# Feed-forward of six batches moved between the attention heads of later batches, with weight preparation in three batches, x in per-batch tiles, and silu written with tanh

## The chip, the cores and the metric

The kernel runs on one core of one Trainium2 chip. The metric is device time in microseconds (us), the median of the runs shown. A profiled execution gives a span (first to last instruction) and the trace that all views below come from.

## The reference

Eight batches of 256 rows, 512 channels, 16 heads of 32 channels; a context of 256 rows per batch. A cross-attention block with int8-like quantised projections, then a feed-forward (FFN) block with fp8-like quantised linears and two reorder indices. Cut to what matters:

```
x = x + tanh(g_xattn) * xattn(layernorm(x), ctx, mask, wq, bq, wk, bk, wv, bv, wo, bo)
x = x + tanh(g_ffn)   * ffn(layernorm(x), w_gate, w_up, w_down, up_idx, down_idx)

xattn: q = w8a8(x, wq, bq); k = ctx @ wk.T + bk; v = ctx @ wv.T + bv   # 16 heads
       o = softmax(q k^T / sqrt(32) + mask) v;  return w8a8(o, wo, bo)
w8a8:  rows of x and of w divided by their absmax/127 and rounded, product rescaled
ffn:   qx = fp8(x[:, up_idx] / row scale); g, u = qx @ fp8(W[:, up_idx]).T, rows in down_idx order
       t = silu(g) * u;  qt = fp8(t[:, down_idx] / row scale);  y = qt @ fp8(w_down[:, down_idx]).T
```

The FFN is 512 to 1408 (gate and up) to 512.

## The kernel before

All rows stand in 16 row tiles of 128 (two per batch). The kernel has three stages.

**Prologue.** SP loads context, mask, wk, x, wv, wq, wo; all eight batches of x go into one resident tile `x_sb`. The constants come on ACT's queue, the two gates last. `held_up` builds a 0/1 mask of the columns that `up_idx` names; wk and wv are turned on PE (`prep_fp32`), wq and wo are quantised and turned (`prep_int8`). `project_kv` and `project_q` make keys, values and queries of batch 0. POOL gathers `dd_i` (the doubled index) and marks the columns that `down_idx` names by 11 scattered writes into one DRAM table, `held_d` (`mark_down`, L341).

**Attention.** A loop over 8 batches of 8 steps (two heads a step) plus 8 more steps. Each step runs three parts at lags 0, 1 and 2: `scores` (PE L538; then per head and row tile a fused add-mask-and-minimum on DVE, L553, and an exponential on ACT, L563), `transposed` (four fp32 PE transposes a head, L579, and a copy out of PSUM on DVE L588 or ACT L586) and `products` (PE L597, a copy, a turn back, a scaling on DVE L620). Beside these, `slots` receive other work by `spread`: the next batch's context turns, keys, values and queries (their bias add on POOL, L505), the output projection of the batch before (`project_out`; y on DVE L666, two adds into `x_sb` on POOL L669 and L670), the second layernorm and its quantisation (`quantise_x2`, stored to DRAM as `scr_x`), the layernorm statistics of all later batches (in batch 0), and the "pieces": 11 row blocks each of w_gate and w_up (`prep_up`), 4 of w_down (`prep_down`) and the gathers that reorder them through DRAM. The pieces are spread over seven batches. Attention's PSUM is one 4-bank tile for the scores and 4 single banks (`bank`) for everything else.

**Feed-forward.** After the attention pools are closed, a plain loop over 8 batches and two row tiles. POOL gathers the batch's turned rows (`xg`, L834). For each half of the 1408 columns: 16 gate and up matmuls of 352 columns each (L850) into two-bank PSUM tiles; DVE scales gate and up (704 wide, L863 and L872); ACT takes Silu (L881); POOL multiplies into `tt` (L882). Then DVE takes the row's absmax over 1408 (L187), the row is put on the fp8 grid (`fp8_grid`: two ACT passes L165 and L167, two DVE passes L169 and L170), PE turns it (L894), ACT copies it out (L897), 11 matmuls make `yp` (L900), DVE scales (L906), POOL adds x (L907), SP stores. The tiles of this stage have two buffers each.

The queues are not in the order of the source: the language orders each engine's queue by priorities and its own estimates (the mask load of the FFN weights, last in its list of pieces, is issued at 70.1 us). `nc.any` copies go to ACT or DVE by the same choice.

Of the kernel before, what the change touches and what calls it, by code (L numbers as in the profile page):

```python
# [40 lines left out]
P = 128  # L41
# [10 lines left out]
def tile_flamingo_block(  # L52
# [49 lines left out]
    x_sb = ctile([P, NT, C], "x_sb")  # L102

    def load_x(b):
        nc.sync.dma_start(
            x_sb[:, b * TPB : (b + 1) * TPB, :], x[b].rearrange("(t p) c -> p t c", p=P)
        )

    d_i = ctile([P, IC], "d_i", I32)
    nc.scalar.dma_start(d_i, down_idx.rearrange("(k p) -> p k", p=P))  # L110
    u_i = ctile([P, KC], "u_i", I32)
    nc.scalar.dma_start(u_i, up_idx.rearrange("(k p) -> p k", p=P))
# [8 lines left out]
    gate = ctile([P, 2], "gate")  # L121
    nc.scalar.dma_start(gate[:, 0:1], g_xattn.partition_broadcast(P))
    nc.scalar.dma_start(gate[:, 1:2], g_ffn.partition_broadcast(P))
# [27 lines left out]
    md_b = ctile([P, I], "md_b", BF16)  # L151
    mx2 = ctile([P, NT], "mx2")
    var2 = ctile([P, NT], "var2")
# [5 lines left out]
    held_d = dram.tile([I, 1], F32, tag="held_d", name="held_d")  # L159
    scr_x = [dram.tile([C, S], BF16, tag=f"scr_x{b}", name=f"scr_x{b}") for b in range(B)]  # L160

    def fp8_grid(rp, src, rs, dst, n, name):

        v = rp.tile([P, n], F32, tag="r_v", name=f"v_{name}")
        nc.scalar.activation(v, src, AF.Identity, scale=rs)  # L165
        a = rp.tile([P, n], FP8, tag="r_a", name=f"a_{name}")
        nc.scalar.activation(a, v, AF.Abs, scale=0.5, saturate=False)  # L167
        q = rp.tile([P, n], FP8, tag="r_q", name=f"q_{name}")
        nc.vector.tensor_scalar(q, v, F8_MAX, -F8_MAX, ALU.min, ALU.max, saturate=False)  # L169
        nc.vector.scalar_tensor_tensor(dst, a, F8_MAX / 2, q, ALU.max, ALU.mult)  # L170
# [18 lines left out]
    with ExitStack() as actx:  # L189
# [4 lines left out]
        rp = actx.enter_context(tc.tile_pool(name="rp", bufs=2))  # L194
        one = actx.enter_context(tc.tile_pool(name="one", bufs=1))
# [4 lines left out]
        def bank(name, dt=F32):  # L200
# [4 lines left out]
        mv1 = wp.tile([P, NT, 2], F32, tag="mv1", name="mv1")  # L205
        rstd1, nmean1, sx, rsx, qa, qb = (
            wp.tile([P, NT], F32, tag=n, name=n)
            for n in ("rstd1", "nmean1", "sx", "rsx", "qa", "qb")
        )

        def norm_stats(t):
            st = sm.tile([P, 6], F32, tag="st", name=f"st1_{t}")
            nc.vector.bn_stats(st, x_sb[:, t, :])
            nc.vector.bn_aggr(mv1[:, t, :], st)

        def norm_rstd(t0, t1):
            ts = slice(t0, t1)
            nc.vector.tensor_scalar(rstd1[:, ts], mv1[:, ts, 1], LN_EPS, None, ALU.add)
            nc.scalar.activation(rstd1[:, ts], rstd1[:, ts], AF.Sqrt)
            nc.vector.reciprocal(rstd1[:, ts], rstd1[:, ts])  # L220
            nc.vector.tensor_scalar(nmean1[:, ts], mv1[:, ts, 0], -1.0, None, ALU.mult)

        def norm_max(t):
            xc = rp.tile([P, C], F32, tag="r_v", name=f"xc_{t}")
            nc.scalar.activation(xc, x_sb[:, t, :], AF.Identity, bias=nmean1[:, t : t + 1])
            absmax(sx[:, t : t + 1], xc)

        def norm_scales(t0, t1):
            ts = slice(t0, t1)
            nc.vector.tensor_tensor(sx[:, ts], sx[:, ts], rstd1[:, ts], ALU.mult)  # L230
            nc.vector.tensor_scalar(sx[:, ts], sx[:, ts], R127, Q_EPS, ALU.mult, ALU.max)
            nc.vector.reciprocal(rsx[:, ts], sx[:, ts])
            nc.vector.tensor_tensor(qa[:, ts], rsx[:, ts], rstd1[:, ts], ALU.mult)
            nc.vector.tensor_tensor(qb[:, ts], qa[:, ts], nmean1[:, ts], ALU.mult)

        def norm_steps(t0, t1):
            steps = [partial(norm_stats, t) for t in range(t0, t1)]
            steps += [partial(norm_rstd, t0, t1)]
            steps += [partial(norm_max, t) for t in range(t0, t1)]
            return steps + [partial(norm_scales, t0, t1)]  # L240
# [32 lines left out]
        def round_int8(src, rs, dst, name):  # L273
            w = rp.tile([P, C], F32, tag="r_w", name=f"ri_{name}")
            nc.vector.tensor_scalar(w, src, rs, MAGIC, ALU.mult, ALU.add)
            nc.vector.tensor_scalar(dst, w, -MAGIC, None, ALU.add)
# [45 lines left out]
        def held_up():  # L322

            iota = one.tile([P, C], F32, tag="xm", name="iota")
# [13 lines left out]

        def mark_down(k):

            nc.gpsimd.indirect_dma_start(  # L341
                out=held_d[:, :],
# [5 lines left out]
        def load_down_marks():  # L348
            md_f = one.tile([P, I], F32, tag="wd", name="md_f")
            nc.sync.dma_start(md_f, held_d.rearrange("c e -> (c e)").partition_broadcast(P))  # L350
            nc.vector.tensor_copy(md_b, md_f)
# [28 lines left out]
        def prep_down(k):  # L380
            wr = one.tile([P, I], F32, tag="wd", name=f"wd_{k}")
            nc.sync.dma_start(wr, w_down[k * P : (k + 1) * P, :])
            nc.vector.tensor_tensor(wr, wr, md_b, ALU.mult)
# [80 lines left out]
        def project_q(b):  # L464
# [4 lines left out]
            def rows():  # L469
                pt = bank(f"qt_{b}", BF16)  # L470
                for nt in range(TPB):
                    t = b * TPB + nt
                    xc = rp.tile([P, C], F32, tag="r_v", name=f"xq_{t}")
                    nc.scalar.activation(  # L474
                        xc,
                        x_sb[:, t, :],
                        AF.Identity,
                        bias=qb[:, t : t + 1],
                        scale=qa[:, t : t + 1],
# [10 lines left out]
                row_bcast(sxb, sx[:, b * TPB : (b + 1) * TPB], f"sx{b}")  # L490
# [20 lines left out]
        def attention(b, qT, kT, v, mk):  # L511
# [4 lines left out]
            o = kv.tile([P, TPB, C], F32, tag="o", name=f"o_{b}")  # L516
# [11 lines left out]
            def scores(i):  # L528
# [18 lines left out]
                for h in heads:  # L547
                    sn = at.tile([P, TPB, L], F32, tag="sn", name=f"sn_{b}_{h}")
                    pr = at.tile([P, TPB, L], F32, tag="pr", name=f"pr_{b}_{h}", bufs=6)
# [84 lines left out]
        def project_out(b, o):  # L634
# [19 lines left out]
            def product(nt):  # L654
# [10 lines left out]
                y = rp.tile([P, C], F32, tag="r_v", name=f"y_{t}")  # L665
# [3 lines left out]
                nc.gpsimd.tensor_tensor(x_sb[:, t, :], x_sb[:, t, :], bo_b, ALU.add)  # L669
                nc.gpsimd.tensor_tensor(x_sb[:, t, :], x_sb[:, t, :], y, ALU.add)  # L670
# [3 lines left out]
        def quantise_x2(b):  # L674

            xT = one.tile([P, KC, S], BF16, tag="x2T", name=f"x2T_{b}")

            def rows(nt):
                t = b * TPB + nt
                st = sm.tile([P, 6], F32, tag="st", name=f"st2_{t}")  # L680
                nc.vector.bn_stats(st, x_sb[:, t, :])
                mv = sm.tile([P, 2], F32, tag="mv", name=f"mv2_{t}")
                nc.vector.bn_aggr(mv, st)
                nc.vector.tensor_copy(var2[:, t : t + 1], mv[:, 1:2])
                xm = one.tile([P, C], F32, tag="xm", name=f"xm_{t}")
                nc.vector.scalar_tensor_tensor(
                    xm, x_sb[:, t, :], mv[:, 0:1], mu_b, ALU.subtract, ALU.mult
# [3 lines left out]
                rs = scale_of(sm, mx, mx2[:, t : t + 1], f"x2_{t}")  # L691
# [9 lines left out]

        cr, mk = load_batch(0)
        rows_k = load_halves("k", wk, "o")
        load_x(0)
        rows_v = load_rows("v", wv, "pT", 6)
        rows_q = load_rows("q", wq, "pr", 6)
        two = one.tile([P, 2, C], F32, tag="wd", name="wr_o01")
        nc.sync.dma_start(two, wo[: 2 * P, :].rearrange("(k p) c -> p k c", p=P))
        rows_o = [two[:, 0, :], two[:, 1, :]]
        for k in (2, 3):  # L710
            wr = ld.tile([P, C], F32, tag="wr", name=f"wr_o{k}", bufs=2)
            nc.sync.dma_start(wr, wo[k * P : (k + 1) * P, :])
            rows_o.append(wr)
        for b in range(1, B):
            load_x(b)
        held_up()
        prep_fp32("k", rows_k)
        for f in norm_steps(0, TPB):
            f()
# [22 lines left out]
        nc.gpsimd.dma_start(held_d.rearrange("(k p) e -> p (k e)", p=P), zeros)  # L742

        def gate_piece(k):
            mark_down(k)
            prep_up("gate", w_gate, k)

        pieces = [partial(gate_piece, k) for k in range(IC)]
        pieces += [partial(gather_up, "gate")]
        pieces += [partial(prep_up, "up", w_up, k) for k in range(IC)]  # L750
        pieces += [partial(gather_up, "up"), load_down_marks]
        pieces += [partial(prep_down, k) for k in range(KC)] + [gather_down]

# [6 lines left out]

        parts = {}
        for g in range(B * NP + NP):
            b, i = divmod(g, NP)
            if i == 0:
# [3 lines left out]
                if b == 0:  # L768
                    spread(slots, norm_steps(TPB, NT), 0, 4)
                    spread(slots, [out_scales], 5, 6)  # L770
                if b + 1 < B:
                    cr, mk = load_batch(b + 1)
                    kT, v, kv_steps = project_kv(b + 1, cr)
                    qT, q_steps = project_q(b + 1)
                    spread(slots, kv_steps, 0, 6)
                    spread(slots, q_steps, 4 if b == 0 else 3, 7)
                if b > 0:
                    spread(slots, project_out(b - 1, o_last) + quantise_x2(b - 1), 2, NP)
                if b < B - 1:
                    n0, n1 = (len(pieces) * k // (B - 1) for k in (b, b + 1))  # L780
                    spread(slots, pieces[n0:n1], 4 if b == 0 else 0, NP)
# [6 lines left out]


    with ExitStack() as fctx:  # L790
        fp = fctx.enter_context(tc.tile_pool(name="fp", bufs=1))
        fx = fctx.enter_context(tc.tile_pool(name="fx", bufs=3))
        fw = fctx.enter_context(tc.tile_pool(name="fw", bufs=2))
        fs = fctx.enter_context(tc.tile_pool(name="fs", bufs=4))
        ps_g = fctx.enter_context(tc.tile_pool(name="ps_g", bufs=1, space=PSUM))
        ps_q = fctx.enter_context(tc.tile_pool(name="ps_q", bufs=2, space=PSUM))
        ps_y = fctx.enter_context(tc.tile_pool(name="ps_y", bufs=2, space=PSUM))

        def row_bcast_f(dst, cols, name):
# [160 lines left out]
```

## Time and profile before

| | us |
|---|---|
| median of 3 runs (751.19 to 754.42) | 753.54 |
| profiled execution, device time | 751.51 |
| its span | 749.7 |
| mean granted TensorE clock | 0.869 |

| engine | busy us | instructions |
|---|---|---|
| PE (matmul) | 529.4 | 3565 |
| DVE (vector) | 550.4 | 1437 |
| ACT (scalar) | 415.6 | 956 |
| POOL (GpSimd) | 272.2 | 237 |

The first scores of the attention run on PE at 55.06 us, the last exponential starts at 495.8, the first FFN matmul at 521.3 and the last store is issued at 741.0. Busy time is the union of an engine's instructions; "idle before X, released by Y" says what ended a gap.

### The profile page before, as it was taken

The page shows a single profiled execution, that of the slowest core. Times are in us where ns is not written, and L with a number is a line of the kernel's source. Part 1 is how long each engine was busy: PE and PEld are TensorE (multiplying, and loading weights), DVE is VectorE, ACT ScalarE, POOL GpSimd, SP SyncE. Part 2 cuts the span into 40 slices and gives each one's busy share as a digit, 9 for nine tenths or more (in the row PEclk, how much of TensorE's full clock was granted, in tenths as well). Part 3 has the DMA queues.
Part 4 walks back from the last instruction along what each step waited for, and adds up shares of the span by engine and source line. Part 5 has one row for each costly group of instructions (what it writes and reads, how often), then busy time and mean ns, then how long its engine had stood idle before and what let it go on. Part 6 is the DMA issues. An engine that isn't in the chain of part 4 may idle for free. (4 is left out here: it accounts for less than half of the span.)

```text
span 749.7 us, 10414 instructions
## 1 busy us (share of the span) xinstructions
PE 529.4 (71%) x3565; PEld 341.6 (46%) x3588; DVE 550.4 (73%) x1437; ACT 415.6 (55%) x956; POOL 272.2 (36%) x237
## 2 busy tenths in 40 slices
PE   1637877878967787887867765643857767777762
PEld 1524645646646545555545444431634434444421
DVE  2755978699797788797689873755567676968971
ACT  1436877768657658678486553552235444545550
POOL 5154046035144224131301115104455576655440
PEclk9879888989989889989998888766689899989985
DMA  8931112002043012012311123000100010000000
GB/s 242 239 108 41 68 43 85 1 29 86 1 138 115 15 41 73 2 46 89 120 53 39 40 78 92 1 15 14 43 14 32 25 42 29 33 24 29 29 14 28
DMA packets 26853, 42.32 MB, mean 56 GB/s; under 512 B 6352, under 2 KB 13904, under 8 KB 26800
## 3 DMA queue, kind: packets, MB, share of 16 engines
q1 hardware_dynamic: 18512, 28.91, 12.0%
q0 software_dynamic: 4704, 12.21, 5.7%
q10 hardware_dynamic: 3584, 0.54, 0.5%
q8 instruction: 28, 0.46, 0.2%
q14 instruction: 25, 0.20, 0.1%
HBM read 31.02 MB, written 10.63 MB: 56 GB/s over the span
## 5 line engine op out<-in xcount | busy, mean ns | idle before, releaser
L563 ACT ACTIVATE pr<-sn,nm 128x256 f32<-128x256 f32 x256 | 128.4, 506 | 51.0 <-DVE nm L553 39.0
L553 DVE CUSTOM_DVE_ANT_0 sn<-s,mk 128x256 f32<-128x256 f32 x256 | 98.4, 417 | 24.4 <-issue 9.5
L579 PE MATMUL t<-ident,pr 128*128 128x128 f32 x512 | 83.8, 314 | 11.3 <-DVE pT L588 4.2
L850 PEld LDWEIGHTS <-xg 128*128 128x128 bf16 x512 | 52.6, 104 | 74.7 <-issue 35.0
L882 POOL TENSOR_TENSOR tt<-up,sl 128x704 f32<-128x704 f32 x32 | 62.9, 1966 | 40.0 <-DVE up L872 23.8
L579 PEld LDWEIGHTS t<-ident,pr 128*128 128x128 f32 x512 | 69.1, 164 | 18.1 <-DVE pT L588 4.6
L434 PE MATMUL pk<-cT,wkT 128*128 128x256 f32 x256 | 64.1, 403 | 5.6 <-ACT cT L427 5.4
L505 POOL TENSOR_SCALAR qT<-qT,bq_c 128x256 f32<-128x256 f32 x32 | 16.7, 524 | 139.5 <-DVE qT L502 139.3
L850 PE MATMUL p_up<-upT,xg 128*128 128x352 bf16 x256 | 51.9, 340 | 20.9 <-DVE up L872 18.3
L450 PE MATMUL pv<-wvT,cT 128*128 128x512 f32 x128 | 61.5, 627 | 0.0
L850 PE MATMUL p_gate<-gateT,xg 128*128 128x352 bf16 x256 | 49.0, 336 | 14.4 <-DVE gs L863 7.7
L434 PEld LDWEIGHTS pk<-cT,wkT 128*128 128x128 f32 x256 | 50.4, 204 | 12.9 <-ACT cT L427 5.6
L538 PE MATMUL s<-kT,qT 32*128 32x256 f32 x512 | 42.0, 439 | 18.6 <-POOL qT L505 11.1
L588 DVE COPY pT<-t 128x512 f32<-128x512 f32 x64 | 43.9, 686 | 9.9 <-PE t L579 6.4
L187 DVE TENSOR_REDUCE mxt<-tt 128x1 f32<-128x1408 f32 x16 | 25.9, 1620 | 33.7 <-POOL tt L882 33.7
L563 ACT ACTIVATION_READ_ACCUMULATOR pr<-sn,nm 128x1 f32 x256 | 49.4, 193 | 0.0
L586 ACT COPY pT<-t 128x512 f32<-128x512 f32 x64 | 37.1, 579 | 18.3 <-PE t L579 13.5
L897 ACT COPY qtT<-ptq 128x1024 bf16<-128x1024 bf16 (+1 forms) x32 | 22.3, 748 | 43.7 <-PE ptq L894 42.1
L900 PE MATMUL yp<-wdT,qtT 128*128 128x512 bf16 x161 | 42.4, 411 | 5.2 <-ACT qtT L897 3.1
L165 ACT ACTIVATE v_t<-tt,rs_t 128x1408 f32<-128x1408 f32 x16 | 23.5, 1470 | 39.8 <-DVE sy L904 39.8
L669 POOL TENSOR_TENSOR x_sb<-x_sb,bo_b 128x512 f32<-128x512 f32 x16 | 21.3, 1336 | 58.2 <-ACT xq L474 58.0
L597 PE MATMUL poT<-pT,v 128*32 128x256 f32 x512 | 41.0, 446 | 1.8 <-DVE pT L588 1.1
(192 smaller groups left out, 1165.8 us busy)
## 6 DMA issues: line engine op xcount, KB each, us to landing
cr<-in_ctx_dram SPq DMA_DIRECT2D x8, 512.0 KB
x_sb<-in_x_dram SPq DMA_DIRECT2D x8, 512.0 KB
out_dram<-yo SPq DMA_DIRECT2D x16, 256.0 KB
wd<-in_L_ffn_w_down_dram SPq DMA_DIRECT2D x4, 704.0 KB
mk<-in_mask_BxSxS_ff_dram SPq DMA_DIRECT2D x8, 256.0 KB
scr_x<-x2T SPq DMA_DIRECT2D x8, 256.0 KB
scr_gate<-gateT SPq DMA_DIRECT2D x1, 1408.0 KB
scr_up<-upT SPq DMA_DIRECT2D x1, 1408.0 KB
```

The source lines that it names most:

```text
L434: nc.tensor.matmul(pk[:, :L], wTf["k"][:, cc, oc * P : (oc + 1) * P], cT[:, cc, :], start=(cc == 0), stop=(cc == KC - 1),)
L450: nc.tensor.matmul(pv, cT[:, cc, lt * P : (lt + 1) * P], wTf["v"][:, cc, :], start=(cc == 0), stop=(cc == KC - 1),)
L538: return nc.tensor.matmul(pss[h][:, nt, :], qT[r0 : r0 + D, oc, nt * P : (nt + 1) * P], kT[r0 : r0 + D, oc, :], start=True, stop=True,)
L553: nc.vector.tensor_tensor_reduce(out=sn[:, nt, :], in0=pss[h][:, nt, :], in1=mk[:, nt, :], scale=-1.0, scalar=3.0e38, op0=ALU.add, op1=ALU ...
L563: nc.scalar.activation(pr[:, nt, :], sn[:, nt, :], AF.Exp, bias=nm[:, nt : nt + 1], scale=-1.0, accum_out=sums[:, nt, h : h + 1],)
L579: nc.tensor.transpose(pst[:, lc, nt * P : (nt + 1) * P], pr[:, nt, lc * P : (lc + 1) * P], ident,)
L586: nc.scalar.copy(pT, pst)
L588: nc.vector.tensor_copy(pT, pst)
L597: return nc.tensor.matmul(poT[oc][r0 : r0 + D, :], v[0][:, lc, h * D : (h + 1) * D], probsT[h][:, lc, :], start=(lc == 0), stop=(lc == LC ...
L850: nc.tensor.matmul(ph[n][:, j, :QI], xg[:, k, nt * P : (nt + 1) * P], wT[n][:, k, c0 : c0 + QI], start=(k == 0), stop=(k == KC - 1),)
L882: nc.gpsimd.tensor_tensor(tt[:, cols], up, sl, ALU.mult)
L900: nc.tensor.matmul(py, qT[:, k, :], wdT[:, k, :], start=(k == 0), stop=(k == IC - 1))
```

## The change

- **Feed-forward.** The closing stage is gone. `feed_forward(b)` returns 21 steps: one gather, and for each of two row tiles four quarter units of 352 columns, the scale, three grid chunks, the turn, and the down product. The steps of batches 0 to 5 are spread over attention batches 3 to 7; those of batch 6 go into the eight closing steps; those of batch 7 follow. They take PSUM from attention's 4 single banks, and `tt`, `qt`, `qtT` and `xg` have one buffer each.
- **Silu.** A half-scaled gate g/2 goes through Tanh on ACT; POOL adds one, multiplies by g/2 and multiplies by up: three POOL instructions of 352 columns per unit in place of one of 704 per half.
- **Pieces** are spread over batches 0 to 2; the scale broadcasts that opened the old FFN stage become pieces too. `mark_down` writes 11 separate tables, cleared by 11 SP DMAs; `held_down` reads them back as 11 rows and counts them on PE.
- **x** is in four rotating batch tiles loaded two batches ahead. After `project_out` the updated x goes to DRAM (`x1_d`, 16 stores) and comes back for the FFN's last add (16 loads).
- **Layernorm** statistics and both square roots are made batch by batch (`norm_roots`).
- Buffers: `r_v` has four slots shared by more tiles, `pr` five for six, `o` one for two, `x2T` shares the slots of `qxT`. The gates are loaded first on ACT's queue.

The diff, cut:

```
-    x_sb = ctile([P, NT, C], "x_sb")
+    gate = ctile([P, 2], "gate")          # now ahead of the other constants
...
+        def load_x(b):
+            xt[b] = ld.tile([P, TPB, C], F32, tag="x", name=f"x_{b}", bufs=4)
+            nc.sync.dma_start(xt[b], x[b].rearrange("(t p) c -> p t c", p=P))
...
+        def norm_roots(b1, b2):
...
+            nc.scalar.activation(ra, ra, AF.Sqrt)
+            nc.vector.reciprocal(ra, ra)
+            if b2 >= 0:
+                s_x = row_tile(b2, "s_x", 2)
+                nc.vector.scalar_tensor_tensor(
+                    s_x[:, :TPB], norm2[b2][:, TPB:], UNIT, r[:, TPB:], ALU.mult, ALU.mult
+                )
+                nc.vector.tensor_scalar(s_x[:, TPB:], s_x[:, :TPB], 0.5, None, ALU.mult)
...
-                out=held_d[:, :],
+                out=held_d[k][:, :],
...
+        def held_down():
+            hd = fw.tile([P, I], F32, tag="tt", name="held_rows", bufs=1)
+            for k in range(IC):
+                nc.sync.dma_start(hd[k : k + 1, :], held_d[k].rearrange("c e -> e c"))
...
+                nc.sync.dma_start(x1_d[b][nt * P : (nt + 1) * P, :], xt[b][:, nt, :])
...
+        def feed_forward(b):
...
+                def unit(j):
+                    if j == 0:
+                        h["tt"] = fw.tile([P, I], F32, tag="tt", name=f"tt_{t}", bufs=1)
+                    cols = slice(j * QI, (j + 1) * QI)
+                    ph = {}
+                    for n in ("gate", "up"):
+                        ph[n] = bank(f"p_{n}_{t}_{j}")[:, :QI]
+                        for k in range(KC):
+                            nc.tensor.matmul(
+                                ph[n],
+                                xg[0][:, k, nt * P : (nt + 1) * P],
+                                wT[n][:, k, cols],
...
+                    for n, at0 in (("gate", TPB), ("up", 0)):
+                        scaled[n] = fw.tile([P, QI], F32, tag=f"f_{n}", name=f"{n}_{t}_{j}")
+                        nc.vector.scalar_tensor_tensor(
+                            scaled[n], ph[n], s_x[:, at0 + nt : at0 + nt + 1],
+                            sw_b[n][:, cols], ALU.mult, ALU.mult,
+                        )
+                    th = fw.tile([P, QI], F32, tag="th", name=f"th_{t}_{j}")
+                    nc.scalar.activation(th, scaled["gate"], AF.Tanh)
+                    nc.gpsimd.tensor_scalar(th, th, 1.0, None, ALU.add)
+                    nc.gpsimd.tensor_tensor(th, th, scaled["gate"], ALU.mult)
+                    nc.gpsimd.tensor_tensor(h["tt"][:, cols], th, scaled["up"], ALU.mult)
...
+                def down():
+                    x1 = ld.tile([P, C], F32, tag="wr", name=f"x1_{t}", bufs=2)
+                    nc.sync.dma_start(x1, x1_d[b][nt * P : (nt + 1) * P, :])
...
+                steps = [partial(unit, j) for j in range(4)] + [scales]
+                return steps + [partial(grid, s0, n) for s0, n in ICH] + [turned, down]
+            return [gather] + [f for nt in range(TPB) for f in row_tile_steps(nt)]
...
+            if k == 0:
+                for table in held_d:
+                    nc.sync.dma_start(table.rearrange("(p k) e -> p (k e)", p=P), zeros)
...
+        PB = 3
+        ahead = [f for b in range(B - 2) for f in feed_forward(b)]
...
-                if b < B - 1:
-                    n0, n1 = (len(pieces) * k // (B - 1) for k in (b, b + 1))
-                    spread(slots, pieces[n0:n1], 4 if b == 0 else 0, NP)
+                if b < PB:
+                    n0, n1 = (len(pieces) * k // PB for k in (b, b + 1))
+                    spread(slots, pieces[n0:n1], 2 if b == 0 else 0, NP)
+                elif b < B:
+                    n0, n1 = (len(ahead) * (k - PB) // (B - PB) for k in (b, b + 1))
+                    spread(slots, ahead[n0:n1], 0, NP)
+                else:
+                    spread(slots, feed_forward(b - 2), 0, NP)
...
-        for b in range(B):
-            xg = fx.tile([P, KC, S], BF16, tag="xg", name=f"xg_{b}")
...
-                    nc.scalar.activation(sl, gs, AF.Silu)
-                    nc.gpsimd.tensor_tensor(tt[:, cols], up, sl, ALU.mult)
...
+        for f in [partial(norm_roots, B, B - 1)] + feed_forward(B - 1):
+            f()
```

## The prediction

> **What bounds the kernel now.** I read the page's engine line first, then the engines' busy time in stretches, then who waits for whom.
>
> ```profile
> PE 529.4 (71%) x3565; PEld 341.6 (46%) x3588; DVE 550.4 (73%) x1437; ACT 415.6 (55%) x956; POOL 272.2 (36%) x237
> ```
>
> No engine is full over the span; the average hides five stages:
>
> ```profile
> core 0: us, PE busy (x) PEld busy (x) DVE busy (x) ACT busy (x) POOL busy (x), PEclk, DMA share, GB/s
> 0.00:55.00 55.00, 21.85 (x120) 17.73 (x120) 28.44 (x91) 16.99 (x28) 23.84 (x31) 0.88 0.74 196
> 55.00:420.00 365.00, 288.20 (x2142) 195.82 (x2148) 299.59 (x960) 255.90 (x697) 109.73 (x109) 0.91 0.18 56
> 420.00:515.00 95.00, 58.62 (x392) 37.41 (x395) 59.12 (x181) 44.83 (x126) 15.79 (x17) 0.74 0.14 44
> 515.00:540.00 25.00, 15.53 (x77) 10.36 (x76) 12.96 (x30) 7.24 (x10) 14.71 (x14) 0.64 0.15 43
> 540.00:690.00 150.00, 110.32 (x646) 61.98 (x655) 114.19 (x137) 67.82 (x71) 87.73 (x56) 0.91 0.08 29
> ```
>
> Attention with pieces (55 to 420) keeps DVE 82% and PE 79% busy. From 420 to 515 the filler has run out and DVE is at 62%; the handover to the FFN (515 to 540) has it at 52%; steady FFN is at 76%, 12 absmaxes (tile `mxt`) in 150 us, so 12.5 us a row tile. Three waits matter (the first from 540 to 690, the others over the whole run):
>
> ```profile
> DVE mxt L187 <- POOL tt L882: 28.8, 12, 4.6
> ...
> PEld s L538 <- POOL qT L505: 11.8, 2, 11.4
> ...
> DVE sxb L319 <- PE rb_sx L312: 10.2, 5, 2.2
> ```
>
> In the FFN, DVE stands 2.4 us a tile until POOL has made `tt`. In the prologue the first scores wait 11.4 us for `qT`, which DVE had made by 43 us: it is queued on POOL behind markings that wait for one another and two gathers. In attention DVE's gaps are small and mostly end with PE.
>
> **What the Trainium skill says.** (1) ScalarE: Activation LUTs, Table sets: exp and tanh are in one set, sqrt in another, and every switch loads a table. Loads here take 1283 ns, as the page says; that tanh rides with exp no row here shows. (2) SBUF — State Buffer, Who interferes with whom: POOL and a DVE instruction with two SBUF inputs, or in a 2-port mode, exclude each other for the whole instruction. The trace agrees:
>
> ```profile
> 639.13 1.27 DVE L169 TENSOR_SCALAR q_t<-v_t 128x1408 fp8e4<-128x1408 f32 x1
> ...
> 639.60 2.33 POOL L882 TENSOR_TENSOR tt<-up,sl 128x704 f32<-128x704 f32 x1
> ...
> 641.17 2.23 DVE L170 SCALAR_TENSOR_TENSOR qt<-a_t,q_t 128x1408 bf16<-128x1408 fp8e4 x1
> ```
>
> POOL takes 2.33 where its shortest is 1.67, and the DVE grid step behind it 2.23 where its shortest is 1.62. (3) TensorE: Matmul & The Clock Gate, Part 1: the array runs at half clock after idling. Agrees: 0.64 at the handover, 0.91 in the full stages.
>
> **The change, part by part.** First the work per unit. Attention's DVE is 299.6 + 59.1 = 358.7; the pieces' DVE rows add to 88, and all DVE rows exceed its busy time by 1/0.89 because small instructions overlap, so 79. That leaves 280, or 34.9 a batch. PE likewise: 346.8 less 16 for the pieces' turns is 331, or 41.3 a batch. A row tile of FFN, from 540:690 over 12: DVE 9.5, PE 9.2, ACT 5.7, POOL 7.3.
>
> ```profile
> L872 DVE SCALAR_TENSOR_TENSOR up<-p_up,s_x,sb_up 128x704 f32<-128x704 f32 x32 | 30.1, 942 | 0.4 <-PE p_up L850 0.4
> L502 DVE SCALAR_TENSOR_TENSOR qT<-pq,s_q,sxb 128x256 f32<-128x256 f32 x32 | 15.1, 477 | 0.7 <-PE pq L495 0.6
> L906 DVE SCALAR_TENSOR_TENSOR yo<-yp,sy,sd_b 128x512 f32<-128x512 f32 x16 | 11.9, 745 | 10.5 <-PE yp L900 10.5
> ```
>
> *DVE per tile.* Scaling at 352 columns lies between 477 (256) and 745 ns (512): 577. Eight of them are 4.62 us where four of 942 were 3.77: +0.85. The turned copies (ACT, 1.01 + 0.48 us) become `any`; half on DVE is +0.5. Three grid chunks meet POOL's lock more often than one: +0.6 (bounds 0 and 1.5). So 9.5 becomes 11.5. Per batch the separate roots and scales add some seven small instructions of 0.15: +1.
>
> *POOL per tile.* 704 columns take 1.69 us and 512 1.28 (medians), so 352 about 0.94; tensor_scalar at 256 takes 0.46 to 0.52, so about 0.68. A unit is 0.68 + 2 × 0.94 = 2.55, a tile 10.2 where it was 3.4 to 3.9. In batches 3 to 7 POOL then has 12 × (10.2 + 1.3 for the last add + 2.3 of gather issues) + 5 × 7 = 200 us: covered as throughput, not as latency.
>
> *ACT.* Eleven roots, each with a table there and back, against seven loads now: 16 more × 1.28 = 20 us; four tanh of 352 for two Silu of 704 and six short grid passes for two add about 1 a tile. ACT at some 70% hides it in attention; without that cover a switch delays the exponentials by 2.6 us.
>
> *DMA.* 54 more SP issues (16 stores and 16 loads of x, 11 clears, 11 row loads) at 0.33 to 0.37 are 20 us of issue beside a DMA share of 0.18. I cost them at nothing; a reload stuck behind a mask load that waits for its buffer delays only a tile's last add. At worst some 2 us in each of 8 batches. The 11 clears and marks are independent now; POOL's 11 issues stay.
>
> *Prologue.* Separate tables end the marks' waits for one another, and the gates no longer hold two `oh` compares 6.0 us. First scores at 47 instead of 55: −8 (bounds −13, and 0 if POOL still takes weight gathers ahead of `qT`).
>
> *Batches 0 to 2.* DVE 3 × 35.9 + 79 + 4 (scale broadcasts, moved here) = 191; PE 147. At the 83% that this mix shows: 230 us.
>
> *Batches 3 to 7 with 12 tiles.* DVE 5 × 35.9 + 12 × 11.5 = 317; PE 5 × 41.3 + 12 × 9.2 = 317. Both full together. I take 84%: no stretch with thin filler is left, and PE's clock gains, but four banks now serve 69 uses a batch instead of 43, and DVE meets POOL's latency. 377 us, less 12 because batch 7's own output projection and quantising (DVE 10) fall behind it.
>
> *Tail.* Four tiles with single buffers. POOL's 10.2, then absmax and scales (2.0), then three ACT grid passes before `tt` is free (about 3): with overlap 14.5 a tile, against 12.5 now. 4 × 14.5 = 58; the gather of batch 7 waits for the one `xg` buffer, 5; first unit 4; from the last `tt` to the end 24 (absmax 2, grid 5, turn 2, product 4, scale and add 2, store and close 9). Sum 91.
>
> Span: 47 + 230 + 377 − 12 + 91 = 733, where the profiled execution has 749.7. That execution took 751.5, 1.8 above its span and 2.0 under the median; so 735 beside 753.5. Where the old stage cost 12.5 a tile, a hidden tile must cost less: 317 / 0.84 for five batches leaves (377 − 5 × 35.9 / 0.83) / 12 = 13.4, so hiding alone gives nothing; the gain comes from the two thin stretches that go (95 + 25 us with 48 idle on DVE) and the prologue.
>
> **The rivals.** *Fuller engines.* Stretches of 15 us with DVE and PE both near 90% exist (270 to 285: DVE 14.92, PE 13.29). At 88% and 90%: 217 + 352 give 47 + 217 + 352 − 12 + 91 = 695, so 697. Against it: DVE and PE at equal load in fixed order stop each other.
>
> *POOL late, in DVE's queue (slower).* The absmax now sits in the queue that feeds the softmax. Behind it wait L553, the PSUM copies, and through them PE and ACT. Now it waits 2.4 us a tile with POOL at 1.7 after its last input; the chain becomes 2.55 plus queueing behind gathers. At 2.4 more than the 84% allows, 12 tiles are 29 us: 764; at 4.5 it is 789. It decides from 1.5 us a tile (18 us). For it: POOL's own order put waits there already, and locks lengthen both. Against it: other DVE work can stand between.
>
> *The interleave does not happen.* Single buffers let the FFN drift to the end: five batches at 45 each and 16 tiles of 14.5: 47 + 230 + 225 + 232 + 29 = 763.
>
> **How the numbers follow.** Forecast case 0.42 (715 to 750, its centre 735), fuller engines 0.20 (690 to 715), POOL late 0.30 (750 to 790), no interleave 0.08. About 0.5%, 3.8 us, is what a measurement of this kernel can tell from no change. Between 749.8 and 757.3 lie the edges of the first and third cases, 0.08. Faster: 0.20 + 0.38 = 0.58; slower: 0.34. The range 697 to 785 leaves out the ends of the second and third cases.
>
> **What would show it.** Right: first scores near 47; DVE and PE both above 80% in batches 3 to 7; last exponential near 645; about 90 us after it; tanh without loads of its own, some 22 loads in all. Wrong: DVE waiting over 1.5 us a tile for POOL at the absmax, first exponentials of a batch late behind root tables, or scores of batch 3 beginning after 290.

## The result, and the profile after

The changed kernel takes **898.6 us** (median of 4 runs, 896.3 to 906.7) where the kernel before takes 753.98 on the same chip: a ratio of 1.194, 95% interval 1.185 to 1.203. The profiled execution took 906.7, with a span of 904.9 and a mean TensorE clock of 0.791 (0.869 before). The median lies above the range forecast, 697 to 785. The kernel before takes 744.6 to 754.0 us depending on the chip, so the experiments below are compared by their ratio to it on their own chip.

The page's engine line of the changed kernel, and three of its groups (busy us, mean ns of one | idle of the engine ahead of them and what ended it):

```profile
PE 571.7 (63%) x3571; PEld 364.4 (40%) x3594; DVE 579.7 (64%) x1645; ACT 443.4 (49%) x1066; POOL 395.1 (44%) x396
...
L796 POOL TENSOR_SCALAR th<-th 128x352 f32<-128x352 f32 x64 | 71.4, 1116 | 34.9 <-ACT th L795 26.2
...
L180 DVE TENSOR_REDUCE mxt<-tt 128x1 f32<-128x1408 f32 x16 | 25.9, 1620 | 76.7 <-POOL tt L798 76.7
...
L786 DVE SCALAR_TENSOR_TENSOR gate<-p_gate,s_x,sb_gate 128x352 f32<-128x352 f32 x64 | 37.1, 579 | 29.6 <-POOL th L797 15.0
```

DVE has only 29 us more work than before (550.4), but the span has 155 more. Most of the added time is idleness, not work. The stretches (columns: length, busy us of PE, PEld, DVE, ACT and POOL, clock, DMA share, GB/s) are cut at the first scores, at the scores of batch 3, and at the last exponential:

```profile
0.00:55.00 55.00, 24.42 (x124) 18.90 (x124) 24.29 (x83) 15.25 (x27) 26.79 (x35) 0.84 0.57 165
55.00:273.00 218.00, 160.35 (x1030) 109.04 (x1032) 171.41 (x514) 139.32 (x353) 82.67 (x78) 0.83 0.26 83
273.00:762.00 489.00, 327.34 (x2116) 206.33 (x2132) 318.61 (x917) 250.01 (x622) 216.82 (x219) 0.80 0.12 39
762.00:905.00 143.00, 59.62 (x307) 30.12 (x310) 65.43 (x134) 38.80 (x67) 68.79 (x67) 0.68 0.08 26
```

Batches 0 to 2 hold nearly all the pieces (the last of w_down slip into batch 3) and run DVE at 79%. Batches 3 to 7 hold the feed-forward: DVE 65%, PE 67%. The tail after the last exponential is at 46% and 42%. Who waits for whom in batches 3 to 7 (total us, times, longest):

```profile
DVE mxt L180 <- POOL tt L798: 56.2, 11, 8.6
...
PE tb_t L306 <- DVE qt L163: 42.5, 12, 13.4
...
DVE yo L834 <- PE yp L828: 26.9, 10, 5.3
```

All three are steps of one row tile waiting for its previous step. DVE's two are 83 of the 170 us that it stands idle there; the rest is spread over many small waits. The timeline of one tile in the tail shows why such a wait stops everything (start, length, engine, operation; in brackets the idle time ahead and its releaser; other instructions left out):

```profile
855.43 0.93 POOL L798 TENSOR_TENSOR tt<-th,up 128x352 f32<-128x352 f32 x1
...
856.39 1.62 DVE L180 TENSOR_REDUCE mxt<-tt 128x1 f32<-128x1408 f32 x1 [5.55 <-POOL tt L798]
...
861.07 1.21 PE L306 MATMUL tb_t<-ident_b,qt 128*128 128x128 bf16 x8 [15.05 <-DVE qt L163]
...
863.78 4.05 PE L828 MATMUL yp<-wdT,qtT 128*128 128x512 bf16 x10 [0.68 <-ACT qtT L309]
...
867.67 0.76 PE L775 MATMUL p_gate<-gateT,xg 128*128 128x352 bf16 x4
...
867.87 0.75 DVE L834 SCALAR_TENSOR_TENSOR yo<-yp,sy,sd_b 128x512 f32<-128x512 f32 x1 [4.37 <-PE yp L828]
...
869.93 1.09 POOL L796 TENSOR_SCALAR th<-th 128x352 f32<-128x352 f32 x1
```

Read it as a relay. POOL ends `tt` at 856.4; absmax, grid, turn and down product follow, one engine at a time. The next tile's first gate matmuls stand behind this down product in PE's queue (867.67), though their input was there; its first DVE scaling stands behind `yo`; POOL adds x to `yo` and starts the next tile at 869.9. From absmax to POOL's start 13.5 us, POOL's four units 12.3 us (3.07 each), and the next absmax is at 882: **26 us a tile**, with hardly any overlap. The other three distances between absmaxes in the tail are 28, 33 and 30 us, so the mean is 29; this one is the shortest.

### The profile page after: what moved, and what is told of

Same layout as the page of the kernel before. It is cut to its first block, busy times and chain, and to the rows that moved or that the text cites. A ratio compares the mean times of both kernels' runs of the same rounds, so it can differ in the third digit from the quotient of the medians.

```text
span 904.9 us, 11148 instructions
## 1 busy us (share of the span) xinstructions
PE 571.7 (63%) x3571; PEld 364.4 (40%) x3594; DVE 579.7 (64%) x1645; ACT 443.4 (49%) x1066; POOL 395.1 (44%) x396
## 4 chain that ended last, share of the span: by engine, by line
PE 26%; POOL 21%; DVE 21%; issue 15%; ACT 10%; DMA 4%; ACTq 1%; another core or an unknown queue 1%; POOLq 0%; DVEq 0%
PE yp L828 6%; POOL tt L798 5%; POOL th L796 5%; POOL th L797 5%; PE pk L473 4%; PE pv L489 3%; PE t L619 3%; DVE mxt L180 3%; DMA wr_gate<-in_L_ffn_w_gate_dram,dd_i 2%; ACT pr L603 2%; DVE sn L593 2%; POOL xg L752 2%; PE poT L637 2%; DVE qt L163 1%; ACT v_t L158 1%
## 5 line engine op out<-in xcount | busy, mean ns | idle before, releaser
L795 ACT ACTIVATE th<-gate 128x352 f32<-128x352 f32 x64 | 31.8, 497 | 118.8 <-DVE gate L786 87.4
L796 POOL TENSOR_SCALAR th<-th 128x352 f32<-128x352 f32 x64 | 71.4, 1116 | 34.9 <-ACT th L795 26.2
L473 PE MATMUL pk<-cT,wkT 128*128 128x256 f32 x256 | 71.6, 437 | 17.4 <-ACT cT L466 8.1
L835 POOL TENSOR_TENSOR x<-x,yo 128x512 f32<-128x512 f32 x16 | 20.4, 1276 | 141.1 <-DVE yo L834 140.7
L619 PEld LDWEIGHTS t<-ident,pr 128*128 128x128 f32 x512 | 73.8, 171 | 11.9 <-DVE qT L542 4.3
L306 PE MATMUL tb_t<-ident_b,qt 128*128 128x128 bf16 x176 | 25.0, 301 | 83.3 <-DVE qt L163 81.8
L180 DVE TENSOR_REDUCE mxt<-tt 128x1 f32<-128x1408 f32 x16 | 25.9, 1620 | 76.7 <-POOL tt L798 76.7
L828 PE MATMUL yp<-wdT,qtT 128*128 128x512 bf16 x163 | 60.7, 537 | 6.3 <-ACT qtT L309 5.2
L158 ACT ACTIVATE v_t<-tt,rs_t 128x512 f32<-128x512 f32 (+1 forms) x48 | 31.0, 675 | 67.3 <-DVE rs_t L169 44.0
L797 POOL TENSOR_TENSOR th<-th,gate 128x352 f32<-128x352 f32 x64 | 60.3, 942 | 4.8
L798 POOL TENSOR_TENSOR tt<-th,up 128x352 f32<-128x352 f32 x64 | 59.8, 935 | 4.3
L786 DVE SCALAR_TENSOR_TENSOR gate<-p_gate,s_x,sb_gate 128x352 f32<-128x352 f32 x64 | 37.1, 579 | 29.6 <-POOL th L797 15.0
```

Source lines behind the costliest of these rows:

```text
L180: nc.vector.tensor_reduce(dst, src, AX.X, ALU.max, apply_absolute_value=True)
L473: nc.tensor.matmul(pk[:, :L], wTf["k"][:, cc, oc * P : (oc + 1) * P], cT[:, cc, :], start=(cc == 0), stop=(cc == KC - 1),)
L619: nc.tensor.transpose(pst[:, lc, nt * P : (nt + 1) * P], pr[:, nt, lc * P : (lc + 1) * P], ident,)
L796: nc.gpsimd.tensor_scalar(th, th, 1.0, None, ALU.add)
L797: nc.gpsimd.tensor_tensor(th, th, scaled["gate"], ALU.mult)
L798: nc.gpsimd.tensor_tensor(h["tt"][:, cols], th, scaled["up"], ALU.mult)
```

## The experiments

The theories: (A) POOL's three operations a unit are late in DVE's queue; (B) the order of the queues makes a tile's steps a relay; (C) single buffers do so; (D) the rest of the change costs (pieces in three batches, batchwise layernorm with its root tables, fewer buffers); (E) interleaving as such.

**Undo the interleave, keep the rest** (theory D against A, B, E). The FFN goes back to a closing stage as before, with two buffers, Silu and one POOL multiply.

```
-        ahead = [f for b in range(B - 2) for f in feed_forward(b)]
...
+            nc.scalar.activation(sl, gs, AF.Silu)
+            nc.gpsimd.tensor_tensor(tt[:, cols], up, sl, ALU.mult)
```

> The changed kernel with the feed-forward taken out of the attention loop and run as the old closing stage (two buffers, Silu, one POOL multiply per half, x reloaded from DRAM); pieces in three batches, x in batch tiles, per-batch layernorm roots stay. Theory A (the loss sits in the feed-forward's serial chain standing inside the in-order queues): first scores near 55, attention batches after the third back to about 50 us each, last exponential near 500, closing stage 230 to 240, total 735 to 765. Rival B (pieces in three batches, the x round trip and the root tables cost the time): total stays above 800.

Measured: 775.15 against 744.59, ratio 1.043 (1.039 to 1.047), a little above the 735 to 765 us expected. First scores at 47, last exponential at 519, and 12.0 us a tile over the 16 absmaxes of the closing stage, where the kernel before has 11.9. (The prediction's 12.5 is of its first 12 tiles; below, the mean over all 16 is used.) So some 15 of the 19 points come with the interleaved feed-forward as it was written (its order, tanh, POOL's operations and single buffers together), and 4 with the rest.

**One POOL operation, then none, instead of three** (A). The (th + 1) * gate becomes one DVE instruction; in the second kernel the last multiply goes to DVE too.

```
-                    nc.gpsimd.tensor_scalar(th, th, 1.0, None, ALU.add)
-                    nc.gpsimd.tensor_tensor(th, th, scaled["gate"], ALU.mult)
-                    nc.gpsimd.tensor_tensor(h["tt"][:, cols], th, scaled["up"], ALU.mult)   # second kernel
+                    nc.vector.scalar_tensor_tensor(th, th, 1.0, scaled["gate"], ALU.add, ALU.mult)
+                    nc.vector.tensor_tensor(h["tt"][:, cols], th, scaled["up"], ALU.mult)   # second kernel
```

> The changed kernel with (th+1)*gate as one DVE scalar_tensor_tensor; POOL keeps the last multiply. DVE +64 x 0.57 = 37 us, POOL -64 x 2.03 = 130 us. Theory A1 (POOL's three operations make the chain that DVE's absmax, 4.8 us a tile, waits for): absmax waits fall under 20 us, tail period per tile falls from 26-29 to 17-20, total 780 to 830. Rival A2 (single buffers and in-order queues stall whatever POOL costs): waits move to other places, total 870 to 900. Rival A3 (DVE work is the limit): slower than 900.

> As the run with one POOL operation, but the last multiply into tt is on DVE too: DVE +64 x 1.1 = 72 us, POOL has none of the feed-forward's elementwise work. Theory A1: absmax follows its input on one engine and never waits; total 790 to 840, DVE above 650 busy. A2: 870 to 900. A3: above 930.

Measured: 1.114 (1.107 to 1.121) and 1.104 (1.100 to 1.109). One wait of each kernel, over its whole run (total us, times, longest):

```profile
DVE mxt L180 <- POOL tt L799: 20.6, 12, 4.6
```

```profile
DVE yo L835 <- PE yp L829: 45.6, 14, 4.8
```

The absmax's wait falls from 76.7 to 20.6 us, then to none, although DVE's work rises from 580 to 608 and 624 us. POOL is worth some 9 points. But DVE still waits 45.6 us for `yp` (50.0 in the changed kernel), and a tile in the tail takes 25 and 24 us in the mean where it took 29 (17 to 20 were expected of the first kernel): half the loss is elsewhere.

**All of the feed-forward after attention** (E against A, B, C), with the steps, buffers and POOL operations of the change.

```
-                elif b < B:
-                    n0, n1 = (len(ahead) * (k - PB) // (B - PB) for k in (b, b + 1))
-                    spread(slots, ahead[n0:n1], 0, NP)
...
+        for b in range(B):
+            for f in feed_forward(b):
+                f()
```

> The changed kernel with all eight batches' feed-forward steps put after the attention loop, with their single buffers, tanh and three POOL operations. Theory A: attention ends near 500 (last exponential), and the 16 tiles take 26 to 29 us each as they do in the tail of the changed kernel, 415 to 465 in all: total 920 to 970, so the interleaved tiles were hidden only in small part. Rival B: attention ends after 600. Rival C (the tail's 26 to 29 is a matter of the last batches alone): tiles take 15 us, total 760.

Measured: 1009.78, ratio 1.357 (1.351 to 1.363), more than the 920 to 970 us expected. A tile takes 27.6 us with nothing beside it (16 absmaxes from 570.4 to 983.7). Its waits over the whole run:

```profile
PE tb_t L306 <- DVE qt L163: 256.0, 32, 17.8
...
DVE mxt L180 <- POOL tt L798: 112.4, 16, 9.0
...
DVE yo L834 <- PE yp L828: 70.0, 16, 4.8
```

Per tile PE stands 16 us for the grid, DVE 7.0 for POOL and 4.4 for the down product. The relay is a property of the new steps, not of attention beside them; interleaving hides part of it (1.194 against 1.357) and can't hide all.

**Is it the buffers, the form of silu, or the pieces?** One kernel gives the changed one a second `tt` buffer; three put one part of the change each into the kernel before: single buffers for `xg`, `tt`, `qt`, `qT`; tanh with three POOL operations at 704 columns; the pieces in batches 0 to 2.

```
-                        h["tt"] = fw.tile([P, I], F32, tag="tt", name=f"tt_{t}", bufs=1)
+                        h["tt"] = fw.tile([P, I], F32, tag="tt", name=f"tt_{t}", bufs=2)   # first; x 3 tiles, r_v 3
...
-                tt = fw.tile([P, I], F32, tag="tt", name=f"tt_{t}")
+                tt = fw.tile([P, I], F32, tag="tt", name=f"tt_{t}", bufs=1)     # second; also xg, qt, qT
...
-                    nc.scalar.activation(sl, gs, AF.Silu)
+                    nc.scalar.activation(sl, gs, AF.Tanh)                       # third; + add, two multiplies on POOL
...
-                if b < B - 1:
+                if b < 3:                                                       # fourth
```

> The changed kernel with two buffers for tt (and the weight rows that share its tag); to make room, x has three batch tiles instead of four and r_v three slots instead of four. If the single tt is what makes a tile begin only after the one before has ended: the tail's tiles come down from 26-29 to 15-18 us, and batches 3 to 7 shorten by 40 us or more: total 790 to 840. If the order of the queues or another buffer does it: tail period stays 25 or more, total 880 to 920.

> The kernel before with one buffer each for xg, tt, qt and qT in its closing stage, nothing else changed. If single buffers serialise the tiles: the closing stage goes from 12.5 to 20-25 us a tile, total 860 to 950. If they cost little by themselves: 13 to 15 a tile, total 750 to 790.

> The kernel before with silu by tanh and three POOL operations (704 wide), buffers as they were. POOL per tile: 2 x (2.2 + 2 x 1.69) = 11.2 us by width, or 2 x (2.0 x 1.1 + 3.4) if the one-operation tensor_scalar costs 3.1 ns an element as at 352. If POOL's throughput is the limit, the closing stage is paced by POOL at 12 to 14 us a tile and the total rises by 0 to 30: 745 to 775. If POOL's latency in the chain stalls DVE's queue: 15 to 18 a tile, 790 to 830.

> The kernel before with its weight pieces in batches 0 to 2 instead of 0 to 6. An attention batch without filler took 52 us in the undone kernel and 53 with a seventh of the pieces in the kernel before, so the pieces were free where they lay: batches 0 to 2 should take 70 each and the rest 52, total 18 to 30 us slower. Rival: DVE's sum counts, so the place does not matter, within 5 us of before.

Measured: 1.190 (1.186 to 1.194), 1.030 (1.027 to 1.033), 1.084 (1.081 to 1.088) and 1.003 (1.002 to 1.005). A second `tt` moves next to nothing: the tail still takes 29 us a tile in the mean and 26 at the last, with the same order in PE's queue, the next tile's first gate matmuls right behind the down product:

```profile
845.06 4.46 PE L828 MATMUL yp<-wdT,qtT 128*128 128x512 bf16 x11 [0.28 <-ACT qtT L309]
...
849.35 0.76 PE L775 MATMUL p_gate<-gateT,xg 128*128 128x352 bf16 x4
```

In the kernel before, where the queues overlap two tiles, single buffers cost only some 1.6 us a tile (13.6 for 11.9), and three POOL operations 4.0 (15.9). Neither makes 26. That leaves the order. The pieces cost nearly nothing, against the expectation of 18 to 30 us.

**Order the steps so that tiles overlap** (B). The kernel with two `tt`, with the four units of the next tile written ahead of this tile's scales, grid, turn and down product; then the same without POOL operations.

```
-            return [gather] + [f for nt in range(TPB) for f in row_tile_steps(nt)]
+            return [[gather] + tiles[0][:4], tiles[1][:4]], [s[4:] for s in tiles]
...
+                for front, back in zip(fronts, backs):
+                    out_steps += front
+                    if held_back:
+                        out_steps += held_back.pop()
+                    held_back.append(back)
```

> The run with two buffers for tt, with the steps written so that the four units of the next tile stand ahead of the scales, grid, turn and down product of the tile before. If the order of the queues (next tile's matmuls behind the turn and the down product of this one) is what makes 26 us a tile: the tail's period falls to 15-18, batches 3 to 7 shorten, total 790 to 840 against 887. If POOL's three operations set it: period 20 or more, total 860 to 890.

> As the run with the overlapped tiles, and POOL's three operations on DVE. Both causes gone: tail period 12-15, attention batches with 2.4 tiles 75 to 80 us, total 750 to 785. If the interleave costs by itself (four PSUM banks, in-order queues): 790 to 820, as the run without POOL operations alone (822).

Measured: 1.092 (1.087 to 1.097) and 1.058 (1.052 to 1.063). The order alone, with the second `tt` in place, takes 9.8 points off 1.190; DVE's wait for `tt` over the whole run falls from 77.6 to 17.8 us. Order and POOL's operations overlap: without POOL's operations the same order takes 4.6 points (1.104 to 1.058), and with the order mended POOL's operations are worth 3.4 (1.092 to 1.058), not 9. The filled batches of three kernels, in stretches (same columns, beginning 7 to 14 us ahead of the first scores of batch 3): two `tt`; two `tt` and the new order; and that without POOL operations.

```profile
265.00:750.00 485.00, 327.77 (x2166) 205.58 (x2164) 325.03 (x940) 253.07 (x631) 222.72 (x224) 0.82 0.12 40
```

```profile
265.00:695.00 430.00, 316.74 (x2138) 199.90 (x2148) 337.67 (x929) 250.42 (x629) 222.18 (x217) 0.86 0.14 44
```

```profile
260.00:676.00 416.00, 309.88 (x2145) 197.17 (x2157) 356.30 (x1028) 254.58 (x635) 79.10 (x77) 0.89 0.14 45
```

DVE's share goes from 67 to 79 to 86%: the third is the occupancy that the forecast took for granted. It still doesn't win, because DVE now has 356 us to do there, and 620.8 in all against 566.2 of the undone interleave (1.043). With both faults mended in this way, hiding the feed-forward costs more than a closing stage of 12 us a tile; the 750 to 785 us expected (measured 797.6) did not come. A version with the new order that leaves the units on POOL in a cheaper form (the next experiment) was not run, so it isn't shown that no interleave can win.

**POOL's first operation in its two-operation form.** The add of 1 becomes an add of 1 and a multiply by 1, nothing else.

```
-                    nc.gpsimd.tensor_scalar(th, th, 1.0, None, ALU.add)
+                    nc.gpsimd.tensor_scalar(th, th, 1.0, 1.0, ALU.add, ALU.mult)
```

> The changed kernel with POOL's add of one written as a tensor_scalar of two operations (add 1, multiply by 1). If the one-operation form is slow: the instruction falls from 1.09 to 0.65-0.75 us, POOL 25 us less busy, total 865 to 885. If the width or the in-place write is slow: 1.09 stays or grows, total within 10 us of 890-899.

Measured: 1.138 (1.131 to 1.144), 5.7 points under the change. The instruction by tile (minimum/median/maximum ns), first in the changed kernel, then here:

```profile
L796 POOL TENSOR_SCALAR th<-th x64: 1085/1091/1594, 313.1 to 879.2; 128x352 f32<-128x352 f32 x64
```

```profile
L796 POOL TENSOR_SCALAR th<-th x64: 477/487/938, 302.1 to 833.0; 128x352 f32<-128x352 f32 x64
```

Less than half the time for more arithmetic. 0.60 us by 64 is 39 us of POOL, and the total fell by about 43, to 859.1 us, below the 865 to 885 expected: in this relay POOL's saved time counted whole. Why the one-operation form is slow stays open.

**What is in the remaining 4 points?** (D) To the undone interleave: the old number of buffers (`o` two, `pr` six, own `x2T` and `xm`); then instead without the square root, so that no root table is loaded. The last is the overlapped kernel without POOL operations, also without root.

```
-            o = one.tile([P, TPB, C], F32, tag="o", name=f"o_{b}")
+            o = kv.tile([P, TPB, C], F32, tag="o", name=f"o_{b}")       # first
...
-            nc.scalar.activation(ra, ra, AF.Sqrt)                         # second and third
```

> The kernel with the closing stage put back (775), and attention's buffers as before: two for o, six for pr, x2T and xm in buffers of their own. An attention batch without filler took 52 us there and 42 in the kernel before with its pieces in three batches. If the shared buffers make the 10 us: batches of 42 to 45, total 740 to 752. If the per-batch layernorm with its square-root tables and the x round trip make it: batches of 50 to 52, total 768 to 778.

> The kernel with the closing stage put back, with the Sqrt function left out of norm_roots (one over the variance is used in place of one over its root): no square root and no table of it. If the tables and the waits for the root make the loss of 4%: batches without filler at 42 to 45 us, ratio 1.00 to 1.015. If the per-batch layernorm work and its place make it: ratio 1.03 to 1.045, batches of 48 to 52.

> The kernel with overlapped tiles and no POOL operations in the units (ratio 1.058), with the Sqrt function left out of norm_roots as well. If root tables cost in the full batches too: ratio 1.02 to 1.04. If the full batches are limited by PE and DVE in fixed order: 1.05 to 1.06.

Measured: 1.034 (1.030 to 1.038), 1.032 (1.026 to 1.038) and 1.055 (1.048 to 1.061). The kernels they vary have 1.043 and 1.058, so buffers and roots are worth about a point each, differences between chips included; they were not tried together. Dropping 18 table loads in the third is within the intervals. Its trace has one table load in all, for 64 tanh and 256 exponentials: so tanh does ride with exp, which no row of the kernel before could show. Three batches without pieces show where the rest lies: the kernel before with pieces in three batches (first fence of each pair), then the undone interleave without root. Stretch, and one DVE group in it:

```profile
327.00:453.00 126.00, 113.45 (x931) 78.13 (x928) 102.08 (x361) 93.76 (x278) 21.09 (x25) 1.00 0.07 20
```

```profile
L482 DVE TENSOR_SCALAR qx<-xq 128x512 bf16<-128x512 f32 x6 | 2.3, 421 | 0.0
```

```profile
340.00:490.00 150.00, 122.06 (x934) 84.01 (x935) 122.69 (x424) 100.04 (x291) 22.74 (x25) 0.94 0.09 31
```

```profile
L522 DVE TENSOR_SCALAR qx<-xq 128x512 bf16<-128x512 f32 x6 | 7.8, 1332 | 0.0
```

From first scores to first scores a batch takes 49 us instead of 42, with 6 to 7 us more DVE work: some 3 of layernorm statistics, which the kernel before did once in batch 0, and some 2.5 because `qx` and `xm` are stretched. At those moments POOL adds to x. The Trainium skill (SBUF — State Buffer, Who interferes with whom) says that whichever of the two starts first holds the shared ports for its whole instruction; the 1332 against 421 ns agrees, since all six of these `qx` passes meet an add of POOL that began before them, and none of the other six does. But this lock is not the greater part: with the old buffers no `xm` is stretched and three of the six `qx` take 0.41 us, and those batches still take 50 us. How the rest divides into work, roots and order stays open: no run separates them.

**What the readings are good for.** Two edits to the kernel before. The marks' clearing table is made from the first queries (`qT` times zero), so POOL's marks can't go ahead of them; and the second half's `tt` multiply goes to DVE. The first alone, then both.

```
+         nc.vector.tensor_scalar(zeros, qT[:, 0, :IC], 0.0, None, ALU.mult)
...
-                    nc.gpsimd.tensor_tensor(tt[:, cols], up, sl, ALU.mult)
+                    (nc.gpsimd if half == 0 else nc.vector).tensor_tensor(tt[:, cols], up, sl, ALU.mult)
```

> The kernel before with the marks held until the first queries are done, nothing else. First scores 44 to 48 us in place of 55: ratio 0.985 to 0.99. The rest of the two-edit kernel's 0.962 is then the second half's multiply on DVE.

> The kernel before with two edits: the second half's multiply into tt on DVE (so that the absmax follows on the same engine, where it waits 2.1 us a tile for POOL), and the 11 marks held until the first queries are done (so that POOL's queue has the query bias first). DVE gains 1 us a tile, loses the wait: closing stage 11.5 a tile in place of 12.5, 10 to 16 us; first scores 6 to 10 us earlier: total 722 to 738 against 745. If DVE is the limit of the closing stage, only the marks help: 737 to 745.

Measured: 0.992 (0.989 to 0.995) and **0.962 (0.959 to 0.966)**: 724.4 us where the kernel before takes 753.6, faster than both kernels. First scores come at 43 and 44; the held marks are worth some 0.8 points and the moved multiply the other 3. The closing stage of the second in DVE's timeline, and its steady stretch:

```profile
629.34 0.88 DVE L883 TENSOR_TENSOR tt<-up,sl 128x704 f32<-128x704 f32 x1
630.14 1.61 DVE L170 SCALAR_TENSOR_TENSOR qt<-a_t,q_t 128x1408 bf16<-128x1408 fp8e4 x1
631.67 1.60 DVE L187 TENSOR_REDUCE mxt<-tt 128x1 f32<-128x1408 f32 x1
```

```profile
540.00:696.00 156.00, 122.58 (x769) 69.99 (x782) 142.79 (x180) 83.62 (x89) 70.99 (x49) 0.96 0.10 33
```

The multiply takes DVE 0.88 us where POOL took 1.97 on average; the absmax follows without a wait, DVE is 92% busy, and a tile takes 10.4 us instead of 11.9.

## Why the prediction was wrong, point by point

| | forecast | measured | difference |
|---|---|---|---|
| first scores | 47 | 55 | +8 |
| batches 0 to 2 | 230 | 218 | −12 |
| batches 3 to 7 | 365 | 489 | +124 |
| tail | 91 | 143 | +52 |
| span | 733 | 905 | +172 |

- **Work per unit: right.** DVE 318.6 forecast as 317 in batches 3 to 7, PE 327 as 317; the 352-column scaling 579 ns as 577. That the sums agree so closely is in part luck: the stretch holds 11 whole tiles and part of a twelfth, not 12, and the last w_down pieces, which were counted ahead of it.
- **The 84% occupancy of batches 3 to 7: the step that failed.** The stretch that the forecast read, at 82 to 83%, has many independent pieces as filler; 84% was then given to a filler that is a chain of some ten steps over four engines, written tile after tile. Measured 65%, so the term of 365 us took 489. The order (9.8 points alone) and POOL's operations (9 alone) make most of it, overlapping: with both mended, 13.6 points less and 86%. The four PSUM banks, which the forecast named beside POOL's latency, were not tested apart.
- **The tail's 14.5 us a tile: the same step again.** The text says "with overlap"; nothing in the list of steps gives an overlap, since `turned` and `down` of one tile precede `unit` of the next. 26 to 33 us measured, 29 in the mean. Summing the chain of one tile would have shown it: 12.3 of POOL and 13.5 of the rest.
- **POOL's tensor_scalar: mis-sized.** Taken from the `qT` row (an add and a multiply, 256 columns) as 0.68 us; the one-operation form took 1.09, and the two-operation form at the same width 0.49. A POOL tile is 11.8 us, not 10.2.
- **The rival "POOL late": right mechanism and side, far too small.** Its price ended at 4.5 us a tile, 789 us. The wait came to 56.2 us in 11 tiles, 5.1 each, about what its end had; but the relay beyond POOL (PE waiting up to 13.4 us for the grid, DVE up to 5.3 for `yp`) was in no case. The range therefore missed.
- **"The interleave does not happen" (763): wrong in price.** It used 14.5 a tile; with the whole feed-forward behind attention it took 27.6, and 1010 in all.
- **Batches 0 to 2, the tables, the SP issues: about right, in part by luck.** 218 for 230, but from 171 us of DVE work at 79% where 191 at 83% were forecast: two misses that offset each other. (PE's 147 there does not follow from its stated terms, 3 × 41.3 + 16 = 140; it measured 160.) 19 table loads where some 22 were forecast; leaving the roots out changed nothing that can be told in the overlapped kernel and a point in the undone one. The extra stores and loads do not appear among the long waits.
- **Prologue: right in part.** The marks no longer wait for one another: eight follow at 1.3 us each. But POOL still takes these eight and a weight gather ahead of the first `qT` (50.2; DVE had made it by 46.5), as the forecast's bound of no gain had it. First scores came at 55 here, and at 44 to 53 in other versions with this prologue. The marks begin at 38.7 here and at 32.6 in the kernel with one POOL operation, in the same order; why they begin late here was not looked into. Held marks alone give 43 in the kernel before, so the reading of the old queue was right.
- **"The gain comes from the two thin stretches": not so.** Three batches with no pieces at all ran PE at 90% (113.45 of 126 us) and DVE at 81% at clock 1.00, so lack of pieces alone did not make the old stretch thin; in that kernel too the last batch and what follows it are the thin part (DVE 67% from 453 to 516). Whether any filler could win that back isn't shown: no version here did.

The signs of being wrong: "DVE waiting over 1.5 us a tile" came; "scores of batch 3 after 290" did not (273). Late exponentials behind roots came once: in batch 5 the first of them runs 13.3 us after the first scores, with a root and its two table loads between. In the kernel before, that distance is up to 14.6 us without a root, so no loss can be put down to it. Of the signs of being right, only tanh without loads of its own came, with 19 loads in all.

## What to carry to other kernels

Before pricing a filler by its busy time, write one unit of it as a chain across the engines' queues and ask what of the next unit stands ahead of this one's waits; where the next unit's first steps stand behind this one's last in an engine's queue, as they did here, each unit costs its whole chain. The Trainium skill (Perfetto Trace Analysis, Optimization Strategy) says that interleaving regimes with different limits may help; here the two regimes had the same limit, DVE and PE nearly equal, and no version of the interleave that was run beat the closing stage, even with DVE at 86%. The better use of the same reading was local: take the one wait that ends last in the stage (absmax for POOL) and move half of its producer to the engine that waits.

## What the hardware showed that was not expected

- POOL's tensor_scalar with one immediate operation took 1.09 us on 128x352 fp32 (median of 64), the same instruction with two operations 0.49.
- DVE's `qx` pass (six of them, 128x512) took 1332 ns on average where 421 is usual, when POOL worked on x at the same time.
- Attention without filler kept the clock at 1.00 for 126 us; the relay of the full interleave had 0.80, and 0.68 in its tail. The slower clock goes with the idleness, and the same work takes PE longer: 571.7 us busy where it was 529.4, at 3571 matmul records for 3565, and 537 ns in the mean for a matmul of the down product where it was 411. How much of the lost time this makes was not measured apart.
